# Attention with norms: the activations transposed by transfers and VectorE instead of TensorE

## The chip, the cores and the metric

The kernel runs on one core of a Trainium2 chip. The core has TensorE (PE; its weight loads are listed apart, as PEld), VectorE (DVE), ScalarE (ACT), GpSimd (POOL) and SyncE (SP), whose queue issues all of this kernel's transfers; 16 DMA engines carry them out. SBUF is the on-chip memory of 128 partitions, PSUM the accumulators that TensorE writes. The metric is the device time of one execution in microseconds, as the median of several.

## What is computed

Input `x` is (8, 2048, 512) in float32: 8 sequences of 2048 tokens with 512 features. Of the reference, this is what matters:

```python
N, S, E, H = (4, 2048, 512, 16)
def proj(W, b):
    y = jnp.einsum('nse,fe->nsf', x, W) + b
    return y.reshape(n, s, h, d).transpose(0, 2, 1, 3)
scores = jnp.einsum('nqhd,nkhd->nhqk', Q, K) * scale
attn = jax.nn.softmax(scores, axis=-1)
out = jnp.einsum('nhql,nlhd->nqhd', attn, V)
out = out.reshape(n, s, e)
return jnp.einsum('nse,fe->nsf', out, Wo) + bo
...
x = x + _layernorm(_L0_attn_ref(_layernorm(x, axis=-1), L0_attn_Wq, ...), axis=-1)
x = x + _layernorm(_L0_ffn_ref(_layernorm(x, axis=-1), L0_ffn_attn_mask, ...), axis=-1)
```

Q, K and V come out of `proj` with the heads ahead of the tokens, so the einsums let the 16 heads of a token attend to each other, for each token by itself. In the second line an expert layer gives each of its 16 experts `s_len // n_head` tokens, which is 8 // 16 = 0 for this shape, so what is left of it is a norm with gain `ln_g` and shift `ln_b`. The change touches the beginning alone: x is normed over its features and turned, so that the features lie on the partitions, as the products with Wq, Wk and Wv need it.

## The kernel before

**Units and steps.** The 16384 tokens are worked through in 32 units of 512 tokens, each of 4 tiles of 128 tokens (`NU`, `NT`, `Q4`). Unit `u` has four steps `c` = 0 to 3. While the softmax, the weighing with V and the output rows of unit `u` (and the rows of `u - 1`) are computed, the products q, k and v of unit `u + 1` are made and x of the unit after that is prepared.

**The order is written out by hand.** `STEPS` (lines 692 to 701) has a string for each step, `FIRST_STEPS` (703 to 709) those of the first unit; `step` (712) goes through the items from left to right and each issues its instructions. Every engine, SP's queue with them, executes its own instructions in that order, each when what it waits for is there. The waits follow from the tiles: a tile of a pool with `bufs` buffers takes the place of an older one when all that read the older one is done. The first unit has its own list (`first_unit`, 597), the last one too (`LAST`, 774).

**x before the products.** `lx` loads a tile of 128 tokens (`load_x`, line 243); `xs` takes its mean and variance on VectorE and the reciprocal root on POOL (`stat_x`, 183/184 and 190/191); `xn` norms it on VectorE and sets the last feature to 1 on POOL (`norm_x`, 260/261); `px` turns it in four 128 x 128 transposes on TensorE into a PSUM bank (`turn_x`, 267); `xa` copies the bank into `xb` on ScalarE (`keep_x`, 279/281); `xt`, for the third and fourth tile of a unit, makes four differences, two on VectorE and two on POOL (`add_x`, 290 to 293). `xb` holds seven operands of a product scheme with seven products in place of eight.

**The products.** `q1` to `q7`, `k1` to `k7`, `v1` to `v7` (`multiply`, 317) and `d1` to `d7` for the output (`out_multiply`, 507) are eight matmuls each. Products 1, 6, 7 and 4 of a letter add up in one PSUM bank ("a"), and between them the bank is copied out as it stands: `1e`, `6e`, `7e`, `4e` (`collect` 331 to 350 on ScalarE, `out_collect` 516 on ScalarE and 519 on VectorE). Products 5 and 3 share another bank, and 2 has its own; `2e`, `5e`, `3e` (353, 521) are on VectorE. `w` items write a part to DRAM by SP (`write`, 364/367), from where `sq`, `sk`, `sv` read it back in another layout into qd, kx and vd (376, 382).

**The softmax in a step.** `mx` takes the maximum and the difference on VectorE (404, 406) and the exponential on ScalarE (414); `dn` the sum and its reciprocal on VectorE (419, 420) and the scaling on POOL (421); `tr` transposes 32 x 32 blocks on VectorE (426); `x0` to `x3` place it in `ex` on ScalarE (431); `sc` and `av` are the small products of TensorE at the end of a step (393, 442); `ok` copies the weighed values out (453), `ou` lays the mask (133).

**The rows in a step.** `lr` loads residual rows r by SP (469) for the next step's `ra`; `rs` at the end of a step takes the sum of squares on ScalarE (543) and the reciprocal root on POOL (190/191) for the next step's `ra`; `ra` (552), `rv` (moments of r), `rg` (562), `rf` (566) and `rt` (moments) follow on VectorE, the roots on POOL; `re` takes an offset on VectorE (577), norms on ScalarE (584) and adds on POOL (588); `st` stores by SP (589). `sB` and `sA` are sums on POOL (476 to 480), `ds` seeds a bank on ScalarE (494).

Step 1 before, as an example of the strings:

```python
        "lx lr q6 q6e mx ra dn ok ou q5 rv q7 tr q7e x0 x1 x2 x3 k1 rg rf q5e k1e rt q4 xs q3 q4e re k2 q3e xn"
        " q5w q4w rs px st xa q3w k2e sc av",
```

## Time and profile before

| | |
|---|---|
| three runs | 1883.60, 1885.58, 1885.72 us; median 1885.58 |
| profiled execution | span 1882.1 us from its first to its last instruction; no time of its own beside the span is listed |
| TensorE | 98% busy; 24,026 matmuls |
| VectorE, ScalarE, GpSimd | 76%, 62%, 55% busy |
| clock granted to TensorE | 0.995 of full speed on average |
| DMA | 63% of the 16 engines' time; 312.58 MB in 370,051 packets |
| x's transposes (line 267) | 512 on TensorE, 281 ns each as a row |
| x's norms (line 260) | 128 on VectorE, 740 ns each |
| x's copies (279, 281) | 64 of 595 ns and 64 of 503 ns on ScalarE |
| x's differences (290 to 293) | 128 of some 420 ns on VectorE, 128 of some 737 ns on POOL |

A row of the profile's groups names a line, an engine, an operation and what it writes and reads, then how often it ran, its busy time in all and the mean of one in ns, and at its end the engine's idle time just before and who ended it. A matmul's end is modelled, so two that follow each other overlap in the rows; what one costs the path is read from the chain of work that ended last, which gives each piece the time until the next. A transfer's row on SP is its issue alone; the time to landing is listed apart. In the view by stage each line is a stretch of time: its length, then each engine's busy time and (x) number of instructions in the order PE, PEld, DVE, ACT, POOL, then the granted clock, the DMA engines' busy share and GB/s.

### The profile page before, as it was taken

To read this page: it belongs to the slowest core of one execution; us is meant where nothing else is said; L and a number is where in the kernel's file an instruction comes from. 1 tells how busy PE (TensorE), PEld (TensorE's weight loads), DVE (VectorE), ACT (ScalarE), POOL (GpSimd) and SP (SyncE) were. 2 spreads that over 40 slices of the span, in tenths; PEclk is the share of its full clock that TensorE was granted. 3 is DMA by queue.
4 is the path that set the end of the run, shared out by engine and by line. 5 is a ranking of instruction groups with operands and counts; after the bars stand their busy time and mean duration, and the time that the engine had idled before them with its cause. 6 is when DMAs were issued, how large, how long until landed. Compare 5 with 4: busy or idle time off the path is not lost.

```text
span 1882.1 us, 57927 instructions
## 1 busy us (share of the span) xinstructions
PE 1847.4 (98%) x24026; PEld 1596.9 (85%) x24026; DVE 1423.8 (76%) x2634; ACT 1172.4 (62%) x1910; POOL 1028.9 (55%) x1785
## 2 busy tenths in 40 slices
PE   8999999999999999999999999999999999999994
PEld 7888888888888888888888888888888888888872
DVE  7667777777777777777777777777777777777777
ACT  2556566666666665666666666566666656666666
POOL 5345654555554565555556545555545555455546
PEclk9999999999999999999999999999999999999998
DMA  7765766566766657665667665576556677656671
GB/s 218 187 158 154 186 174 162 152 167 166 181 169 161 166 147 191 175 162 150 171 157 185 172 163 161 154 181 180 161 158 168 157 189 193 165 147 163 154 186 57
DMA packets 370051, 312.58 MB, mean 166 GB/s; under 512 B 149750, under 2 KB 280825, under 8 KB 365564
## 3 DMA queue, kind: packets, MB, share of 16 engines
q1 hardware_dynamic: 369788, 308.89, 63.0%
q8 instruction: 188, 3.08, 0.7%
q14 instruction: 75, 0.61, 0.1%
HBM read 174.59 MB, written 135.27 MB: 165 GB/s over the span
## 4 chain that ended last, share of the span: by engine, by line
PE 93%; POOL 2%; DVE 1%; ACT 1%; DMA 1%; issue 1%; SPq 0%; POOLq 0%; ACTq 0%; DVEq 0%
PE paq L317 12%; PE pak L317 12%; PE pav L317 11%; PE pad L507 11%; PE pk L317 9%; PE pq L317 9%; PE pv L317 9%; PE pd L507 8%; PE sa L393 6%; PE sa L442 4%; PE px L267 3%; ACT ex L431 1%; POOL rs_d L191 1%; POOL e L421 0%; POOL rs_d L190 0%
## 5 line engine op out<-in xcount | busy, mean ns | idle before, releaser
L431 ACT COPY ex<-eT 32x512 f32<-32x512 f32 x512 | 315.5, 616 | 40.1 <-DVE eT L426 31.2
L421 POOL TENSOR_TENSOR e<-e,den 128x512 f32<-128x512 f32 x128 | 134.6, 1052 | 323.2 <-DVE den L420 265.4
L191 POOL TENSOR_TENSOR rs_d<-rs_d,nhalf 128x1 f32<-128x1 f32 x384 | 211.1, 550 | 32.0
L588 POOL TENSOR_TENSOR a<-a,r 128x512 f32<-128x512 f32 x120 | 181.7, 1514 | 44.1 <-ACT a L584 27.0
L190 POOL TENSOR_SCALAR rs_d<-mv_d 128x1 f32<-128x1 f32 x250 | 50.1, 200 | 255.9 <-DVE mv_d L184 242.8
L404 DVE TENSOR_REDUCE top<-sa 128x16 f32<-128x512 f32 x128 | 88.7, 693 | 103.5 <-PE sa L442 66.7
L584 ACT ACTIVATE a<-a,nm,rs_d 128x512 f32<-128x512 f32 x120 | 97.7, 814 | 97.2 <-DVE nm L577 97.2
L414 ACT ACTIVATE e<-e 128x512 f32<-128x512 f32 x128 | 80.8, 631 | 122.7 <-DVE e L406 122.5
L453 ACT COPY oT<-sa 128x512 f32<-128x512 f32 x124 | 134.4, 1084 | 31.8 <-PE sa L442 29.6
L260 DVE TENSOR_SCALAR x<-x,mv_x,rs_x 128x512 f32<-128x512 f32 x128 | 94.7, 740 | 53.5 <-POOL rs_x L191 52.8
L419 DVE TENSOR_REDUCE den<-e 128x16 f32<-128x512 f32 x128 | 87.2, 681 | 62.9 <-ACT e L414 62.8
L393 PEld LDWEIGHTS sa<-kx,qd 64*32 64x32 f32 x8192 | 109.2, 139 | 29.9 <-issue 27.7
L133 ACT COPY sa<-under 128x1024 f32<-128x1024 f32 x129 | 131.7, 1021 | 2.1
L426 DVE STREAM_TRANSPOSE eT<-e 128x512 f32<-128x512 f32 x128 | 91.0, 711 | 54.7 <-POOL e L421 54.7
L393 PE MATMUL sa<-kx,qd 64*32 64x64 f32 x8192 | 129.1, 249 | 1.0 <-DMA vs<-cv 0.9
L543 ACT ACTIVATE junk<-a 128x512 f32<-128x512 f32 x120 | 84.1, 701 | 71.7 <-DVE a L521 71.7
L442 PE MATMUL sa<-ex,vd 64*32 64x64 f32 x8192 | 123.2, 226 | 3.9 <-ACT ex L431 3.4
L317 PE MATMUL paq<-xb,sq 128*128 128x256 f32 x512 | 124.2, 386 | 0.1
L317 PE MATMUL pak<-xb,sk 128*128 128x256 f32 x512 | 124.2, 386 | 0.0
L317 PE MATMUL pv<-wv,xb 128*128 128x256 f32 x512 | 124.1, 385 | 0.0
L317 PE MATMUL paq<-xb,wq 128*128 128x256 f32 x512 | 123.2, 384 | 0.7 <-ACT xb L281 0.4
L317 PE MATMUL pav<-wv,xb 128*128 128x256 f32 x512 | 121.2, 380 | 1.0 <-ACT u3v L337 1.0
(163 smaller groups left out, 4719.8 us busy)
## 6 DMA issues: line engine op xcount, KB each, us to landing
qs<-cq SPq DMA_DIRECT2D x128, 256.0 KB, 2.3
qd<-qs SPq DMA_DIRECT2D x128, 256.0 KB, 5.3
ks<-ck SPq DMA_DIRECT2D x128, 256.0 KB, 2.4
kx<-ks SPq DMA_DIRECT2D x128, 256.0 KB, 4.3
vs<-cv SPq DMA_DIRECT2D x128, 256.0 KB, 3.1
vd<-vs SPq DMA_DIRECT2D x128, 256.0 KB, 4.4
r<-in_x_dram SPq DMA_DIRECT2D x128, 256.0 KB, 4.9
x<-in_x_dram SPq DMA_DIRECT2D x124, 256.0 KB, 4.5
```

Source lines behind the costliest of these rows:

```text
L133: nc.scalar.copy(sa, under.unsqueeze(1).to_broadcast([P, 2, UT]))
L191: nc.gpsimd.tensor_tensor(rs, rs, nhalf, ALU.pow)
L260: nc.vector.tensor_scalar(xs[t], xs[t], mv[:, 0:1], rs, ALU.subtract, ALU.mult)
L317: nc.tensor.matmul(ps[:, 256 * m : 256 * m + 256], lhsT=left[:, e, P * m : P * m + P], rhs=right[:, e, :], start=(n in (1, 2, 5) and m == ...
L393: nc.tensor.matmul(sa[32 * i : 32 * i + 32, t, 64 * rh : 64 * rh + 64], lhsT=qd[u][d].rearrange("p h (b m) -> p (h b) m", b=2)[:, :, m], r ...
L421: nc.gpsimd.tensor_tensor(e, e, den.unsqueeze(2).to_broadcast([P, 16, 32]), ALU.mult)
L431: nc.scalar.copy(ex[q, :, i % 2, :], sm["t"][q])
L442: nc.tensor.matmul(o[:, J], lhsT=vd[u][d, 4 * c + rh, J, :], rhs=ex[d, 8 * (J // 2) + 2 * rh + J % 2].rearrange("p i k -> p (i k)"), start ...
L453: nc.scalar.copy(dst, sa[:, :, 256:].rearrange("p t (k h R) -> p t k h R", k=Q4, h=Q4))
L507: nc.tensor.matmul(ps[:, m], lhsT=left[:, e, P * m : P * m + P], rhs=right[:, e], start=(n in (2, 5) and m == 0 and e == 0), stop=(e == 1) ...
L584: nc.scalar.activation(a, a, AF.Identity, bias=nm, scale=rs)
L588: engine.tensor_tensor(a, a, res.pop((u, k)), ALU.add)
```

## The change

x is no longer turned by TensorE, but for the first unit's four tiles. `load_x` deals the 256 tokens of two tiles out in blocks of 32, `norm_x` norms on ScalarE into a lasting tile `xn` (four places; the last feature stays 1 from the start; an offset is taken on POOL first), the new `move_x` (item `xm`) moves a pair of tiles by four transfers from SBUF to SBUF so that each quarter of the features comes to 32 partitions, and `turn_x` (`px`) now is one VectorE transpose of 32 x 32 blocks for the pair, straight into `xb`. The target of the transfers, `px[h]`, is in a pool with one buffer. The differences are taken for 256 tokens at once, in items of their own: `xt` on VectorE, `xp` on POOL. In a unit after the first, `xs` and `xn` of a tile run in every step, two steps before where they ran; `xm` is the first item of step 1 and follows `sk` in step 3; `px` is in step 1, behind `q4`, and in step 2, behind `rt`; in step 1 the transfers of pair `h + 1` stand ahead of the transpose of pair `h`. `q2` in step 0 moves from behind `rf` to behind `d2e`, `sv` to the front of step 0, `xs` to behind `tr`. The features' new order goes into the weights' rows on the host. The kernel asks for less scratch for dynamic transfers.

```diff
+    mpool = ctx.enter_context(tc.tile_pool(name="mpool", bufs=1))
...
+    xn = const.tile([P, 2, 2, E], F32, name="xn")
...
     def load_x(t):
         if t < NT:
             xs[t] = xpool.tile([P, E], F32, tag="x", name=f"x_{t}")
             n, s = divmod(P * t, S)
-            nc.sync.dma_start(xs[t], x[n, s : s + P, :] if t < NT - Q4 else renumbered[t % Q4])
+            if t < Q4:
+                nc.sync.dma_start(xs[t], x[n, s : s + P, :])
+                return
+            s -= P * (t % 2)
+            J = t % Q4 - t % 2
+            src = x[n, s : s + 2 * P, :] if t < NT - Q4 else renumbered[J : J + 2].rearrange("J p e -> (J p) e")
+            nc.sync.dma_start(xs[t], src.rearrange("(b i t) e -> i t b e", b=Q4, i=2)[t % 2])
...
+    def normed(t):
+        return xn[:, t // 2 % 2, t % 2]
+    def norm_first(t):
+        mv, rs = xrs.pop(t)
+        nc.vector.tensor_scalar(
+            normed(t).rearrange("p (k a e) -> p a k e", k=EC, a=Q4),
+            xs.pop(t).rearrange("p (a k e) -> p a k e", k=EC, a=Q4),
+            mv[:, 0:1], rs, ALU.subtract, ALU.mult,
+        )
+        nc.gpsimd.memset(normed(t)[:, E - 1 : E], 1.0)
     def norm_x(t):
         if t < NT:
             mv, rs = xrs.pop(t)
-            nc.vector.tensor_scalar(xs[t], xs[t], mv[:, 0:1], rs, ALU.subtract, ALU.mult)
-            nc.gpsimd.memset(xs[t][:, E - 1 : E], 1.0)
-    def turn_x(t):
-        if t < NT:
-            px[t] = ps_pj.tile([P, EC, P], F32, tag="pj", name=f"px_{t}")
-            for ec in range(EC):
-                nc.tensor.transpose(px[t][:, ec, :], xs[t][:, ec * P : (ec + 1) * P], ident)
-            del xs[t]
-    def keep_x(t):
-        if t < NT:
-            u, J = divmod(t, Q4)
-            if J == 0:
-                xb[u] = pool2.tile([P, 7, 2, 2 * P], F32, tag="xb", name=f"xb_{u}")
-            j = slice(P * (J % 2), P * (J % 2) + P)
-            if J < 2:
-                dst = xb[u][:, 0:2].rearrange("p n e t -> p (n e) t")[:, :, j]
-                nc.scalar.copy(dst, px[t])
+            nm = small.tile([P, 1], F32, tag="nm", name=f"nmx_{t}")
+            nc.gpsimd.tensor_scalar(nm, mv[:, 0:1], rs, -1.0, ALU.mult, ALU.mult)
+            nc.scalar.activation(
+                normed(t)[:, 0 : E - 1], xs.pop(t)[:, 0 : E - 1], AF.Identity, bias=nm, scale=rs
+            )
+    def begin_x(u):
+        if u not in xb:
+            xb[u] = pool2.tile([P, 7, 2, 2 * P], F32, tag="xb", name=f"xb_{u}")
+        return xb[u]
+    def turn_first(t):
+        px[t] = ps_pj.tile([P, EC, P], F32, tag="pj", name=f"px_{t}")
+        for ec in range(EC):
+            nc.tensor.transpose(px[t][:, ec, :], normed(t)[:, P * ec : P * ec + P], ident)
+    def keep_first(t):
+        dst = begin_x(0)[:, 2 * (t // 2) : 2 * (t // 2) + 2].rearrange("p n e t -> p (n e) t")
+        nc.scalar.copy(dst[:, :, P * (t % 2) : P * (t % 2) + P], px.pop(t))
+    def move_x(h):
+        if h < NT // 2:
+            px[h] = mpool.tile([P, Q4, 2, P], F32, tag="xm", name=f"xm_{h}")
+            for a in range(Q4):
+                src = xn[:, h % 2, :, P * a : P * a + P]
+                nc.sync.dma_start(px[h][32 * a : 32 * a + 32].rearrange("p b i e -> p (b i e)"), src)
+    def turn_x(h):
+        if h < NT // 2:
+            n = 2 * (h % 2)
+            dst = begin_x(h // 2)[:, n : n + 2].rearrange("p n e (c t) -> p (n e) c t", t=32)
+            nc.vector.transpose(dst, px.pop(h).rearrange("p b i (k e) -> p k (b i) e", k=EC))
+    def add_x(u, engine, j=slice(0, 2 * P)):
+        if u < NU:
+            b11, b21, t1, b22, t2, t3, t4 = (xb[u][:, n, :, j] for n in range(7))
+            if engine is nc.vector:
+                nc.vector.tensor_tensor(t3, b22, t1, ALU.subtract)
+                nc.vector.tensor_tensor(t1, t1, b11, ALU.subtract)
             else:
-                nc.scalar.copy(xb[u][:, 2, :, j], px[t][:, 2:4])
-    def add_x(t):
-        if t < NT and t % Q4 >= 2:
-            u, J = divmod(t, Q4)
-            j = slice(P * (J % 2), P * (J % 2) + P)
-            b11, b21, b22, t1, t2, t3, t4 = (xb[u][:, n, :, j] for n in range(7))
-            b12 = px[t][:, 0:2]
-            nc.vector.tensor_tensor(t3, b22, b12, ALU.subtract)
-            nc.vector.tensor_tensor(t1, b12, b11, ALU.subtract)
-            nc.gpsimd.tensor_tensor(t2, b22, t1, ALU.subtract)
-            nc.gpsimd.tensor_tensor(t4, b21, t2, ALU.subtract)
+                nc.gpsimd.tensor_tensor(t2, b22, t1, ALU.subtract)
+                nc.gpsimd.tensor_tensor(t4, b21, t2, ALU.subtract)
...
-        right = xb[u][:, {1: 0, 2: 1, 3: 2, 4: 6, 5: 3, 6: 4, 7: 5}[n]]
+        right = xb[u][:, {1: 0, 2: 1, 3: 3, 4: 6, 5: 2, 6: 4, 7: 5}[n]]
...
     STEPS = (
-        "lx lr sv st ok sB px mx xa q1 q1e ra d2 ou dn d2e rv d6 d6e tr d5 x0 x1 x2 x3 d7 d7e rg rf q2 rt d5e xs"
-        " d4 q2e re xn d4e d3 d3e rs q2w st sc av",
-        "lx lr q6 q6e mx ra dn ok ou q5 rv q7 tr q7e x0 x1 x2 x3 k1 rg rf q5e k1e rt q4 xs q3 q4e re k2 q3e xn"
-        " q5w q4w rs px st xa q3w k2e sc av",
-        "lx lr k6 k6e mx ra dn ok ou k5 rv k7 tr k7e k2w x0 x1 x2 x3 v1 sq rg k5e rf v1e rt k4 xs k4e k5w k3 re xn"
-        " k3e k4w rs px st xa xt k3w sc av",
-        "sk lx lr v2 mx v2e ra v6 ok v6e dn ou ds v5 rv sA v7 tr x0 x1 v7e x2 x3 d1 rg rf v5e v2w d1e v4 rt xs"
-        " v4e v5w v3 re xn v3e v4w rs px xa xt v3w sc av",
+        "sv lx lr st ok sB mx q1 q1e ra d2 ou dn d2e q2 q2e rv d6 d6e tr xs d5 x0 x1 x2 x3 d7 d7e rg rf rt d5e"
+        " d4 q2w xn re d4e d3 d3e rs st sc av",
+        "xm lx lr q6 q6e mx ra dn ok ou q5 rv q7 tr xs q7e x0 x1 x2 x3 k1 rg rf q5e k1e rt q4 px q3 q4e xn re k2 q3e"
+        " q5w q4w rs st q3w k2e sc av",
+        "lx lr k6 k6e mx ra dn ok ou k5 rv k7 tr xs k7e k2w x0 x1 x2 x3 v1 sq rg k5e rf v1e rt px k4 k4e k5w k3 xn re xt"
+        " k3e k4w xp rs st k3w sc av",
+        "sk xm lx lr v2 mx v2e ra v6 ok v6e dn ou ds v5 rv sA v7 tr xs x0 x1 v7e x2 x3 d1 rg rf v5e v2w d1e v4 rt"
+        " v4e v5w v3 xn re v3e v4w rs v3w sc av",
     )
 
     FIRST_STEPS = (
-        "lx sv mx q1 q1e dn ok ou q2 q2e q6 q6e tr k1 k1e x0 x1 x2 x3 q7 q7e q2w lb xs q5 q5e xn q4 q4e px q5w q4w lo"
-        " xa sc av",
-        "lx k2 mx k2e dn ok ou c4 q3 tr k6 k6e x0 x1 x2 x3 q3e k2w q3w k5 xs cs k7 k7e c0 k5e xn px k5w xa sc av",
-        "lx mx v1 v1e dn ok ou k4 k4e k3 k3e tr k4w k3w sq c1 v2 x0 x1 x2 x3 v2e xs c2 c3 v6 v6e xn wt px xa xt v2w sc av",
-        "sk lx ds v7 v7e mx v5 v5e dn ok ou xs tr v4 v4e xn x0 x1 x2 x3 d1 sA v4w v5w d1e px v3 v3e xa xt v3w lg sc av",
+        "lx lx sv mx q1 q1e dn ok ou px q2 q2e xt xp q6 q6e xs tr k1 k1e x0 x1 x2 x3 q7 q7e q2w xn lb xs q5 q5e xn q4 q4e"
+        " q5w q4w lo sc av",
+        "xm lx k2 mx k2e dn ok ou c4 q3 tr k6 k6e x0 x1 x2 x3 q3e k2w q3w k5 xs cs k7 k7e c0 k5e xn k5w sc av",
+        "xm lx lx mx v1 v1e dn ok ou k4 k4e k3 k3e tr k4w k3w sq c1 px v2 x0 x1 x2 x3 xs v2e xs xn c2 c3 v6 v6e xn wt v2w"
+        " sc av",
+        "sk xm lx ds v7 v7e mx v5 v5e dn ok ou px xs tr v4 v4e xn x0 x1 x2 x3 d1 sA v4w v5w d1e v3 v3e xt xp v3w lg sc av",
...
-            "xs": lambda: stat_x(s + 9), "xn": lambda: norm_x(s + 9), "px": lambda: turn_x(s + 8),
+            "xs": lambda: stat_x(next(x_stat)), "xn": lambda: norm_x(next(x_norm)), "xm": lambda: move_x(next(x_move)),
+            "px": lambda: turn_x(next(x_turn)),
...
-            "xa": lambda: keep_x(s + 8), "xt": lambda: add_x(s + 8),
+            "xt": lambda: add_x(next(x_add), nc.vector), "xp": lambda: add_x(next(x_last), nc.gpsimd),
...
-    x_tiles = iter(range(11, 2 * NT))
+    x_tiles, x_stat, x_norm = (iter(range(n, 2 * NT)) for n in (11, 9, 9))
+    x_move, x_turn = (iter(range(n, NT)) for n in (4, 3))
+    x_add, x_last = (iter(range(1, 2 * NU)) for _ in range(2))
...
-    nc = _bacc.Bacc("TRN2", target_bir_lowering=False, num_devices=1)
+    nc = _bacc.Bacc("TRN2", target_bir_lowering=False, num_devices=1, dynamic_dma_scratch_size=1024)
...
+        if m != "o":
+            w = w.reshape(512, 4, 4, 32).transpose(0, 2, 1, 3).reshape(512, 512)
```

The first unit's list changes to match: its first four tiles keep TensorE and a ScalarE copy (`turn_first`, `keep_first`), the next four take the new way (`move_x(2)` behind `spread_qk(0, "k")`, `turn_x(2)` and `move_x(3)` behind `v7e`), and `stat_x(8)` moves ahead of `v5`.

More of the change, by code (lines that the diff above doesn't have):

```diff
@@ L611, in first_unit @@
         stat_x(1)
-        norm_x(0)
-        turn_x(0)
-        keep_x(0)
+        norm_first(0)
+        turn_first(0)
+        keep_first(0)
         stat_x(2)
-        norm_x(1)
-        turn_x(1)
-        keep_x(1)
+        norm_first(1)
+        turn_first(1)
+        keep_first(1)
         stat_x(3)
-        norm_x(2)
-        turn_x(2)
-        keep_x(2)
-        norm_x(3)
-        turn_x(3)
-        keep_x(3)
+        norm_first(2)
+        turn_first(2)
+        keep_first(2)
+        norm_first(3)
+        turn_first(3)
+        keep_first(3)
         for t in range(4, 8):
@@ L631, in first_unit @@
         less_last("q", nc.vector, (0,))
-        add_x(2)
+        for engine in (nc.vector, nc.gpsimd):
+            add_x(0, engine, slice(0, 128))
         less_last("q", nc.vector, (1,))
-        add_x(3)
+        for engine in (nc.vector, nc.gpsimd):
+            add_x(0, engine, slice(128, 256))
         nc.gpsimd.memset(ex, 0.0)
@@ L657, in first_unit @@
         spread_qk(0, "k")
+        move_x(2)
         stat_x(6)
         run(0, "v2 v2e v2w v6 v6e")
-        turn_x(4)
-        keep_x(4)
         norm_x(6)
-        turn_x(5)
         stat_x(7)
@@ L666, in first_unit @@
         run(0, "v7 v7e")
-        keep_x(5)
         load_x(9)
         norm_x(7)
-        turn_x(6)
-        keep_x(6)
+        turn_x(2)
         load_x(10)
-        add_x(6)
-        turn_x(7)
-        keep_x(7)
+        move_x(3)
+        stat_x(8)
         run(0, "v5 v4 v5e v4e v4w v5w")
-        stat_x(8)
-        add_x(7)
         run(0, "v3 v3e v3w")
```

## The prediction

> **What bounds the kernel now.** I read the busy shares first, then the chain of work that ended last, then the busy time by stage and the timeline of one unit in the steady middle.

> ```profile
> span 1882.1 us, 57927 instructions
> PE 1847.4 (98%) x24026; PEld 1596.9 (85%) x24026; DVE 1423.8 (76%) x2634; ACT 1172.4 (62%) x1910; POOL 1028.9 (55%) x1785
> PE 93%; POOL 2%; DVE 1%; ACT 1%; DMA 1%; issue 1%; SPq 0%; POOLq 0%; ACTq 0%; DVEq 0%
> ```

> TensorE is the path. The next view gives the four steps of one unit (span, then busy time and instructions of each engine, clock, DMA share): TensorE is busy for all of every step, at full clock. Between 400 and 1600 us the waits of TensorE come to one, of 0.2 us. So what leaves TensorE comes off the time, as long as nothing else becomes late.

> ```profile
> 904.18:920.13 15.95, 15.95 (x196) 13.83 (x196) 12.33 (x24) 8.75 (x15) 10.70 (x18) 1.00 0.63 159
> 920.13:934.46 14.33, 14.33 (x189) 12.58 (x189) 10.86 (x20) 9.38 (x16) 5.29 (x11) 1.00 0.30 93
> 934.46:947.05 12.59, 12.59 (x189) 11.05 (x193) 8.61 (x17) 8.57 (x13) 4.08 (x10) 1.00 0.80 212
> 947.05:961.39 14.34, 14.34 (x197) 12.59 (x202) 12.18 (x24) 9.73 (x17) 11.51 (x18) 1.00 0.85 212
> ```

> The profiled execution shows its span alone, 1882.1 us; the three runs have 1883.6 to 1885.72, so 1.5 to 3.6 us lie around it. I add changes to the median, 1885.6.

> **What goes from TensorE.** The chain by time prices a turned tile (start, length, what):

> ```profile
> 905.78 0.59 PE px L267 x4
> 906.37 1.73 PE paq L317 x8
> ...
> 934.09 0.44 PE px L267 x4
> ```

> Three tiles of a unit cost 0.44; the one behind the softmax products 0.59, of which 0.19 comes back, since a product that follows those takes 1.92 and not 1.73. That is 3 x 0.44 + 0.40 = 1.72 us a unit. Units 1 to 29 turn 116 tiles (49.9 us); the eight tiles turned in the first unit give 3.5. Saving: 53.4 us.

> A transpose row lasts 273 to 281 ns, but four advance the path by 0.44. [...]

> **What it costs elsewhere, by amount.** Each unit, VectorE loses four norms (0.74) and four small subtractions (0.42) and gets two transposes (0.71 for 512 columns; 1024 against 512 columns adds 0.53 in the two-operand rows, 1.22 against 0.69; so 1.24) and two subtractions of 512 (0.69): -4.6 + 3.9. ScalarE loses 2 x 0.59 + 2 x 0.50 of copies and gets four norms, priced by L584, the same form, 0.81: +1.0. POOL loses 4 x 0.12 and 4 x 0.73 and gets 4 x 0.30 (L579) and 2 x 1.27: +0.3. SP gets 8 issues of about 0.47 (four vd issues take 1.88). The moves add 63,488 packets of 512 B; at the 51 ns that a packet takes on average (63% of 16 engines' 1882 us over 370,051 packets) that is at most 11 points of DMA share. Not shown before are the wide transpose (between one 512 row, 0.71, and two, 1.42), the norm on ScalarE (between L543, 0.70, and L584) and the transfer from SBUF to SBUF (between qs, 2.3 us to landing, and qd, 5.3). All this fits into the idle time above (VectorE 13.2 of 57.2 us a unit, ScalarE 20.8, POOL 25.6), and the price by amount is nothing; without that cover it would be ScalarE's 1.0. The order is another matter.

> [...]

> **What it costs by order.** Steps begin, by the chain, at 904.18, 920.20, 934.53, 947.05; "into step n" counts from there.

> (a) *Step 0, product d4.* q2 stood between d7 and d4; it goes ahead of d6, so d4 follows d7 in the same bank and must wait until ScalarE has copied the bank out (d7e). The first unit shows this hand-over, with two tiles' transposes in between:

> ```profile
> 41.26 1.89 PE L317 MATMUL pav<-sv,xb 128*128 128x256 f32 x8
> 43.23 0.59 ACT L334 COPY u2v<-pav 128x512 f32<-128x512 f32 x1 [4.60 <-PE pav L317]
> 43.87 1.99 PE L317 MATMUL pav<-sv,xb 128*128 128x256 f32 x8
> ```

> From the product's end (43.15) to the next one's start 0.72; back to back they overlap by 0.16. Price 0.9 (0.7 to 1.1 with the slower restart), 30 times. In the first unit v6 and v7 lose this cover too: 0.9 once.

> (b) *Step 1, q3.* The next tile's moments (0.81 of VectorE) move ahead of q5e, which ended at 929.92; q3, which needs it, starts at 930.64. It ends 0.1 late; with the hand-over 0.2 (0 to 0.5).

> (c) *Step 1, SP.* In step 1 the four transfers of the next pair stand first in SP's queue, but their target is the only buffer, and its old content is read by the transpose that VectorE reaches after rt, late in the same step. So SP waits, and the loads of x and r stand behind. rt ends 10.53 into step 1; the moved moments make it 11.34, the transpose ends at 12.58, four issues end at 14.46, x takes 0.6, r is issued at 15.06 and lands 4.9 later (median; 3.1 to 7.2) at 19.96. The shorter step 1 lasts 14.1, so r is there 5.86 into step 2. Before:

> ```profile
> 935.90 0.60 SPq L469 DMA_DIRECT2D r<-in_x_dram  x1
> 937.43 0.74 DVE L552 SCALAR_TENSOR_TENSOR r<-a,rs_d,r 128x512 f32<-128x512 f32 x1
> 939.17 0.69 DVE L419 TENSOR_REDUCE den<-e 128x16 f32<-128x512 f32 x1 [0.99 <-ACT e L414]
> 942.93 0.68 DVE L353 TENSOR_TENSOR ck<-pk,u3k 128x512 f32<-128x512 f32 x1
> 944.73 1.89 PE L317 MATMUL pk<-xb,wk 128*128 128x256 f32 x8
> ```

> (That r serves step 3; the one for step 2 was issued at 921.35.) VectorE needs it at 2.90 into step 2, and behind it in the same queue stand den, the softmax transpose and k5e, which k3 on TensorE waits for. ra starts at 5.86, den at 6.54 where it was 4.64: 1.90 late. k5e ended at 9.08; plus 0.81 plus 1.90 is 11.79, where k3 would start at 10.36. Price 1.45 with the hand-over; a landing of 3.1 makes it 0, one of 7.2 makes it 3.7.

> (d) *Step 2, POOL.* The two subtractions of a pair now stand as one block of 2 x 1.27 ahead of rs, whose reciprocal root ra of step 3 needs. rt ends 2.29 after k5e's start: 13.40. POOL's root takes 0.91 (14.31), the norm's offset 0.30, ScalarE's norm 0.81 and its output norm 0.81 (16.2), POOL's residual add 1.27, the block 2.55, rs 0.82: 20.9. Step 2 now lasts 12.09 + 1.45, so that is 7.35 into step 3, where ra started at 4.19. The 3.16 pass down VectorE's queue to the softmax transpose and on ScalarE to v7e (ended 9.64, now 12.80), and v4, due at 10.45, waits 2.35. Without (c) the same sum gives 1.86; POOL's add at its slowest row, 1.8, makes it 3; with the norm off this chain it falls to 0.7.

> Moved and covered: x's statistics and norms come two steps sooner on tiles that are loaded two steps before; the transfers of step 1 land by 5.7 into step 2 (14.46 + 5.3 - 14.1) and are turned at 13.4; vd's issues pass x and r in step 0, so that r lands about 12 into step 0 and is needed 3 into step 1; kx waits for the later k3w and lands about 12.8 into step 3, before its use at 16. If step 3 weren't lengthened by (d), 1.1 of that cover would be left. The larger of the DMA's costs is in the landing range of (c).

> In the first unit one more x load stands ahead of vd, on which its first weighing waits: within 1 us, taken as 0. The host's new order of weight rows costs nothing on the chip, and the last unit is the same.

> Sum for units 1 to 29: -1.72 + 0.9 + 0.2 + 1.45 + 2.35 = +3.18; x 29 = 92.2. Unit 30: +0.9. First unit: -3.5 + 0.9. Total +90.5, so **1976 us**.

> **Rivals.**
> - *r comes in time* (quieter queue than the median, or room in step 2): only (a), (b), (d) at 1.86. +1.24 x 29 - 1.7 gives 1920. For it: step 1 has a DMA share of 0.30, and the r loads issued in it landed in 4.2 us. Against: the loads stand behind 0.75 MB just issued.
> - *Faster: VectorE's order has room.* The place is ra in steps 2 and 3. If r lands by 4.0 into step 2 and POOL's rs is done by about 5 into step 3, den isn't held and k3 and v4 are on time; (a) and (b) remain: -0.62 x 29 - 1.7, 1866. For it: VectorE idles 13 of 57 us a unit. Against: my rows miss both points by 1.9 and 2.3 us.
> - *All hidden*: 1885.6 - 53.4 = 1832. It needs d4 not to wait for d7e, though both use one bank.
> - *Worse*: (c) at 3.7 and (d) at 3: +6.1 a unit, 2060.
> - The transposes do leave TensorE; a time near 1885 would mean that stalls of 1.7 a unit took their place.

> **Numbers.** About 0.2% (3.8 us) is what a measurement of this kernel can tell from no change. Forecast 0.50 (1940 to 2010), r in time 0.18, room 0.13, all hidden 0.09, worse 0.07, near 1885 0.03. Faster 0.22, within 0.2% 0.03, slower 0.75. The range leaves out all-hidden and the worst: 1862 to 2010.

> **What would show it.** Right: SP waiting in each step 1 for the transpose of the moved tile; the r load issued after the end of step 1; VectorE idle before ra (L552) in step 2 for r's DMA and in step 3 for POOL's root; TensorE waiting for ScalarE before d4 and v4 and for VectorE before k3; px near 0.1% of the chain. Wrong: TensorE without gaps in steps 2 and 3, or r issued as early as before.

## The result, and the profile after

Before 1884.59 us (four runs, 1883.57 to 1885.72), after **2053.24 us** (four runs, 2050.04 to 2059.08): ratio 1.09, 95% interval 1.0882 to 1.0918. The forecast was 1976, the range 1862 to 2010: the direction was right, the size was not. The lines of the page that answer to those of before:

```profile
span 2049.8 us, 57097 instructions
PE 1857.3 (91%) x23523; PEld 1547.5 (75%) x23530; DVE 1398.8 (68%) x2510; ACT 1191.9 (58%) x1910; POOL 1059.5 (52%) x1723
PE 43%; DVE 19%; POOL 12%; DMA 8%; issue 6%; ACT 6%; SPq 5%; POOLq 0%; DVEq 0%; ACTq 0%
```

TensorE has 496 transposes less to do (503 fewer in the records, of which some are missing) and still is the busiest engine, but no longer the path alone: its share of the chain that ended last falls from 93% to 43%, and VectorE, POOL, the transfers and SP's queue hold 44%. No engine has become the bound; all of them are idle more than before. The same unit by stage (columns as before):

```profile
991.42:1008.26 16.84, 16.16 (x194) 13.44 (x193) 10.81 (x21) 10.28 (x16) 10.51 (x17) 1.00 0.80 205
1008.26:1022.55 14.29, 14.15 (x185) 11.99 (x184) 10.62 (x19) 9.64 (x16) 4.87 (x12) 1.00 0.07 25
1022.55:1036.67 14.12, 12.53 (x177) 10.54 (x177) 9.06 (x17) 7.71 (x13) 5.12 (x10) 1.00 1.04 258
1036.67:1053.06 16.39, 14.17 (x185) 12.00 (x185) 12.41 (x22) 9.23 (x15) 12.17 (x17) 1.00 0.97 198
1098.75:1116.82 18.07, 15.86 (x185) 13.19 (x184) 12.56 (x23) 10.03 (x17) 12.97 (x19) 0.91 0.98 202
```

TensorE now waits 0.7 us in step 0, 1.6 in step 2, 2.2 in step 3. The DMA share of step 1 is 0.07: SP stands in its queue. The last line is step 3 of another unit, 1.7 us longer at a lower clock; more on that below. TensorE's waits over the run (total, times, longest) are headed by the three that the prediction named, v4 on u3v, k3 on k5e and d4 on d7e; the fourth line is the longest wait of SP's queue, that of the transfers (L308):

```profile
PE pav L350 <- ACT u3v L370: 61.9, 30, 2.4
PE pk L350 <- DVE ck L386: 49.1, 29, 2.4
PE pad L540 <- ACT a L549: 20.3, 30, 0.7
SPq L308 <- DVE nm L610: 354.4, 29, 19.4
```

In the changed kernel L308 is a transfer of x, L315 the VectorE transpose that reads what the transfers brought, L252 and L502 the loads of x and r, L585 ra, L452 den, L386 q, k and v's VectorE sums, L621 the row's add, L325/326 the block xp, L350 and L540 the products. The timeline of the unit above (start, length, engine, line) shows the two longer waits from end to end:

```profile
1019.66 1.25 DVE L315 STREAM_TRANSPOSE xb<-xm 128x1024 f32<-128x1024 f32 x1
...
1020.97 2.67 SPq L308 DMA_DIRECT2D xm<-xn  x4
...
1024.35 0.61 SPq L502 DMA_DIRECT2D r<-in_x_dram  x1
...
1029.09 0.75 DVE L585 SCALAR_TENSOR_TENSOR r<-a,rs_d,r 128x512 f32<-128x512 f32 x1 [3.30 <-DMA r<-in_x_dram]
1029.76 0.68 DVE L452 TENSOR_REDUCE den<-e 128x16 f32<-128x512 f32 x1
...
1034.01 0.69 DVE L386 TENSOR_TENSOR ck<-pk,u3k 128x512 f32<-128x512 f32 x1
...
1034.75 1.99 PE L350 MATMUL pk<-xb,wk 128*128 128x256 f32 x8 [1.59 <-DVE ck L386]
...
1039.10 1.28 POOL L621 TENSOR_TENSOR a<-a,r 128x512 f32<-128x512 f32 x1 [1.64 <-ACT a L617]
1040.33 1.27 POOL L325 TENSOR_TENSOR xb<-xb 128x512 f32<-128x512 f32 x1
1041.68 1.27 POOL L326 TENSOR_TENSOR xb<-xb 128x512 f32<-128x512 f32 x1
...
1043.31 0.55 POOL L193 TENSOR_TENSOR rs_d<-rs_d,nhalf 128x1 f32<-128x1 f32 x1
1043.90 0.75 DVE L585 SCALAR_TENSOR_TENSOR r<-a,rs_d,r 128x512 f32<-128x512 f32 x1 [2.20 <-POOL rs_d L193]
...
1049.41 1.99 PE L350 MATMUL pav<-wv,xb 128*128 128x256 f32 x8 [2.22 <-ACT u3v L370]
```

First (c): SP begins the four transfers only 12.7 us into step 1, when the transpose of the pair before has ended (the line of SP's waits names nm, a short VectorE instruction that ends 0.04 after it), r is issued 1.8 into step 2 and VectorE is idle until it lands, then den and k5e follow and k3 starts late. Then (d): POOL does the row's add and the block of two before the root that ra needs, ra starts 7.2 into step 3, v4 2.2 late.

By place in the run the 167.7 us of the two spans are: first unit and what is before it +18.5, units 1 to 29 +148.4, unit 30 +0.9, the end 0.

### The profile page after: what moved, and what is told of

Read it like the earlier page. It is cut to its first block, busy times and chain, and to the rows that moved or that the text cites. A ratio compares the mean times of both kernels' runs of the same rounds, so it can differ in the third digit from the quotient of the medians.

```text
span 2049.8 us, 57097 instructions
## 1 busy us (share of the span) xinstructions
PE 1857.3 (91%) x23523; PEld 1547.5 (75%) x23530; DVE 1398.8 (68%) x2510; ACT 1191.9 (58%) x1910; POOL 1059.5 (52%) x1723
## 4 chain that ended last, share of the span: by engine, by line
PE 43%; DVE 19%; POOL 12%; DMA 8%; issue 6%; ACT 6%; SPq 5%; POOLq 0%; DVEq 0%; ACTq 0%
PE pad L540 8%; PE pd L540 8%; PE paq L350 6%; DMA r<-in_x_dram 6%; PE pv L350 5%; POOL e L454 5%; PE sa L426 4%; SPq L308 4%; PE pav L350 3%; DVE eT L459 3%; DVE den L452 3%; PE pq L350 3%; PE sa L475 3%; PE pk L350 2%; DVE r L585 2%
## 5 line engine op out<-in xcount | busy, mean ns | idle before, releaser
L621 POOL TENSOR_TENSOR a<-a,r 128x512 f32<-128x512 f32 x120 | 155.6, 1297 | 194.6 <-ACT a L617 194.6
L585 DVE SCALAR_TENSOR_TENSOR r<-a,rs_d,r 128x512 f32<-128x512 f32 x120 | 91.4, 762 | 161.6 <-DMA r<-in_x_dram 99.4
L284 ACT ACTIVATE xn<-x,nmx,rs_x 128x511 f32<-128x511 f32 x124 | 100.7, 813 | 156.7 <-POOL nmx L283 155.8
L350 PE MATMUL pav<-wv,xb 128*128 128x256 f32 x512 | 130.2, 399 | 61.9 <-ACT u3v L370 61.9
L350 PE MATMUL pk<-xb,wk 128*128 128x256 f32 x512 | 125.8, 389 | 49.1 <-DVE ck L386 49.1
L350 PEld LDWEIGHTS pav<-wv,xb 128*128 128x128 f32 x512 | 97.4, 195 | 86.4 <-ACT u3v L370 73.9
L350 PEld LDWEIGHTS pk<-xb,wk 128*128 128x128 f32 x512 | 95.8, 192 | 72.9 <-DVE ck L386 60.7
L350 PE MATMUL pv<-wv,xb 128*128 128x256 f32 x512 | 133.0, 405 | 5.3 <-DVE cv L386 4.0
L540 PE MATMUL pad<-wo,oT 128*128 128x256 f32 x480 | 116.5, 386 | 20.3 <-ACT a L549 20.3
L350 PE MATMUL paq<-xb,sq 128*128 128x256 f32 x512 | 125.7, 389 | 4.7 <-POOL xb L325 3.7
L350 PE MATMUL pav<-sv,xb 128*128 128x256 f32 x512 | 123.0, 384 | 5.4 <-ACT u2v L367 4.0
```

Of the source, the lines that this page charges most:

```text
L284: nc.scalar.activation(normed(t)[:, 0 : E - 1], xs.pop(t)[:, 0 : E - 1], AF.Identity, bias=nm, scale=rs)
L350: nc.tensor.matmul(ps[:, 256 * m : 256 * m + 256], lhsT=left[:, e, P * m : P * m + P], rhs=right[:, e, :], start=(n in (1, 2, 5) and m == ...
L540: nc.tensor.matmul(ps[:, m], lhsT=left[:, e, P * m : P * m + P], rhs=right[:, e], start=(n in (2, 5) and m == 0 and e == 0), stop=(e == 1) ...
L585: nc.vector.scalar_tensor_tensor(r, y, rs, r, ALU.mult, ALU.add)
L621: engine.tensor_tensor(a, a, res.pop((u, k)), ALU.add)
```

## The experiments

Theory: the order alone costs the time, through those three waits. Rival 1: the added transfers (32.5 MB, 63,488 packets) slow the traffic. Rival 2: the added work of VectorE, ScalarE and POOL can't be hidden. Diffs show pieces of the strings of `STEPS`; each kernel does the whole computation unless it says otherwise.

**The three placements, one by one and together.**

```diff
e_xm, step 1
- xm lx lr q6
+ lx lr q6
- rt q4 px q3
+ rt q4 px xm q3
e_q2, step 0
- d2e q2 q2e rv
+ d2e rv
- rg rf rt d5e d4 q2w
+ rg rf q2 rt d5e d4 q2e q2w
e_rs, step 2
- k3e k4w xp rs st
+ k3e k4w rs xp st
```

e_xm: 

> Step 1's four transfers stand behind the transpose px instead of at the front, so nothing stands behind their wait in SP's queue; they start as late as before. Theory (three waits that the order makes: d4 on d7e, k3 through the late r, v4 through POOL's block ahead of rs): the wait of k3 (49.1 us over the run, 29 times) goes, with some 0.2 us of restart each, and v4's wait loses 0.5 each; with half of the half-clock windows that is 1975 us (1960 to 2000); r is issued about 1.5 into step 1 and VectorE's wait for r's DMA (99.4 us) goes. Rival 1 (the added transfers themselves, 32.5 MB in 63,488 packets, slow the memory traffic): the same bytes move, 2040 or more. Rival 2 (the added work of VectorE, ScalarE and POOL is the cost): 2045 to 2055.

e_q2: 

> q2 stands between d7 and d4 again. Theory: TensorE's wait for d7e (20.3 us, 30 times 0.7) goes, with 0.2 us of restart each: 2027 us (2015 to 2035). If one cause carries nearly all (the late r or POOL's block): 2045 to 2055. Rivals 1 and 2: 2045 to 2055.

e_rs: 

> In step 2 rs stands ahead of POOL's two subtractions xp. Theory: rs is 2.5 us earlier, ra in step 3 starts near 4.7 us and not 7.2, v7e is in time and v4's wait (61.9 us, 30 times, with 0.2 of restart) goes: 1980 us (1965 to 1995). If the late r carries nearly all, v4 is late all the same: 2040 or more. Rivals 1 and 2: 2045 to 2055.

e_all: 

> The three edits together. Theory: the three waits and the half-clock windows go, what is left is the saving of 53 us and about 0.2 us a unit for q3: 1840 us (1832 to 1860). Rival 1 (transfers): over 1900. Rival 2 (amount of work): over 1885.

Measured: e_xm 1991.63 (ratio 1.0568, 1.0552 to 1.0584), e_q2 2045.31 (1.0853, 1.0835 to 1.0871), e_rs 2007.28 (1.0647, 1.0619 to 1.0676), **e_all 1933.47** (1.0256, 1.0240 to 1.0272). The waits of k3 and d4 are gone where their edits took them away; v4's falls from 61.9 us to 17.4 in e_rs. Steps (c) and (d) are real: 62 and 46 us. But all four stay short of the theory: 78 and 73 us were expected of these two, moving q2 back gave 8 where 26 were expected, and the three together stop 93 us above the theory's figure, on the rivals' side. The waits of e_q2 (the first line) and of e_all (the other two) tell why: other waits stood behind those that went.

```profile
PE pad L540 <- POOL oS L510: 10.5, 15, 0.7
```

```profile
PE pad L540 <- POOL oS L510: 16.1, 23, 0.7
PE pav L350 <- ACT u3v L370: 12.1, 27, 1.0
```

In e_q2: between d2 and d6 q2 had covered POOL's sums sB, which are late themselves (in step 0 the copy of the weighed values, their source, waits for ScalarE's tail of the step before). So the place of q2 was paid for on one side and earned on the other. In e_all v4 still waits, since xt stands ahead of the maximum in step 3.

**Rival 1 by itself.** The kernel before, with as many transfers, about where the change has them:

```diff
b_moves
+    def move_more(h):
+        for a in range(Q4):
+            src = yn[:, h, :, P * a : P * a + P]
+            nc.sync.dma_start(ym[32 * a : 32 * a + 32].rearrange("p b i e -> p (b i e)"), src)
step 1
- q5w q4w
+ q5w ym q4w
step 3
- sk lx lr
+ sk ym lx lr
```

> The kernel before, with the change's eight transfers from SBUF to SBUF a unit added (in step 1 behind q5w, in step 3 behind sk) from a lasting tile of zeros into a tile that nobody reads; nothing waits for them. Rival 1 (the transfers themselves cost the time that the three edits left, 1933 against 1832): 1930 to 1990. Theory (order alone): 1886 (1882 to 1895).

Measured: 1891.96, ratio 1.0036 (1.0023 to 1.0049). The page of this run:

```profile
PE 1845.9 (98%) x24019; PEld 1600.5 (85%) x24026; DVE 1422.9 (75%) x2634; ACT 1171.6 (62%) x1910; POOL 1029.5 (55%) x1786
q1 hardware_dynamic: 435068, 340.36, 74.8%
```

The transfers raise the DMA share from 63% to 75% and cost 7.3 us. Rival 1 is out: the load is small, what hangs on it is not.

**Moving on through the order.** Each of the next kernels adds to the one before.

```diff
e_g = e_all, and (the first unit's second xp goes, as step 0 has it)
- k3 xn re xt k3e
+ k3 xn re k3e
- k4w rs xp st
+ k4w rs st
- v3e v4w rs v3w
+ v3e xt v4w rs v3w
- d2e rv d6
+ d2e rv xp d6
e_gf = e_g, and in steps 1, 2 and 3
- xn re k2 q3e q5w q4w rs st
+ rs xn re k2 q3e q5w q4w st
- k4e k5w k3 xn re k3e k4w rs st
+ k4e rs k5w k3 xn re k3e k4w st
- sA v7 tr
+ sA rs v7 tr
- xt v4w rs v3w
+ xt v4w v3w
e_best = e_gf, and in step 1 (in the first unit px goes behind the softmax transpose, xm behind px)
- tr xs q7e
+ tr q7e
- rt q4 px
+ rt xs q4 px
e_h = e_best, and (the first unit's third xm goes, as step 0 has it)
- sk xm lx lr
+ sk lx lr
- sv lx lr st ok
+ sv lx lr st xm ok
e_hk = e_h, and in step 3
- rv sA rs v7 tr xs x0
+ rv sA v7 tr x0
- v4 rt v4e v5w v3 xn re
+ v4 rt rs xs v4e v5w v3 re xn
e_hkl = e_hk, and in step 0
- rv xp d6 d6e tr xs d5
+ rv d6 d6e tr xs xp d5
```

e_g: 

> The three edits together, and the differences of x moved: xt from the end of step 2 to behind v3e of step 3, POOL's xp to step 0 behind rv. With the three edits TensorE still waits for u3v before v4 (12.1 us, 27 times), since xt stands ahead of the maximum on VectorE in step 3, and for POOL's sums before d6 (16.1 us, 23 times), since xp, two-input adds of 2.9 us, pushes the sums, the roots and with them ScalarE's copy of the weighed values into step 0. Theory: both waits and 0.1 to 0.3 of restart each go: 1895 us (1885 to 1910). Rival 1 (transfers) and rival 2 (amount of work): 1925 or more, since the same work is done.

e_gf: 

> As the kernel of the run before, and rs of steps 1 to 3 moved out of the tail of the step (step 1: ahead of xn; step 2: behind k4e; step 3: behind sA), so that ScalarE's copy of the weighed values in the next step does not queue behind it. Theory: ScalarE's tail of 0.9 us leaves step 0, top starts 0.6 to 0.9 earlier there, 0.1 to 0.3 a unit: 1888 us (1878 to 1900). Rivals 1 and 2: no change against the run before.

e_best: 

> As the kernel of the run before; xs of step 1 back behind rt, so that q5e is not late; and in the first unit xm and px of steps 2 and 3 as in the steady units, px behind the softmax transpose and xm behind px. Theory: q3's lateness (0.3 with restart 0.4 a unit, 29 times) goes, 12 us; of the first unit's 18 us over before, 8 to 15: together 1863 us (1850 to 1875), faster than before by over 0.5%. Rival 1 (transfers): over 1900. Rival 2 (amount): over 1885.

e_h: 

> As the last kernel, with the four transfers of step 3 moved to step 0 of the next unit, behind the store, so that vs is not issued behind them. In the last kernel vs takes up to 4.6 us to issue at the turn of the unit, an instruction load of 16 KB starts late there, and TensorE stands still in the middle of its small products with nothing that it waits for (13.7 us in 4 stalls, up to 5.0 each, a half-clock window behind most). Theory (crowded transfers at the turn of the unit hold instruction loads, vs and vd): these stalls and their half-clock windows (about 20 to 25 us together) go, the mean of step 0 falls from 17.4 to 16.5: 1878 us (1870 to 1888). If the stalls come from elsewhere: 1900. Rival 2 (amount of work): 1900.

e_hk: 

> As the kernel of the run before, with the order of step 3 as in the kernel before the change: xs behind rt, re ahead of xn, and rs behind rt. Theory: POOL's root of rt no longer queues behind the roots of rs and x, so re and xn leave ScalarE by about 2.0 into step 0 and its copy of the weighed values follows at 2.0 where it now starts at 2.8; top at 3.1 instead of 3.9, d6 and d2 are not held (0.4 each): 0.7 to 0.9 a unit, 20 to 26 us: 1854 us (1846 to 1866). Rival 2: no change against the run before.

e_hkl: 

> As the kernel of the run before, with POOL's xp in step 0 behind the root of xs instead of ahead of it, so that rg and rf (1.39 and 1.57 us beside it, 0.72 and 0.76 alone) are not slowed and d5e, which d3 waits for (0.2 us, 14 times), is earlier. Theory: 0.1 to 0.2 a unit, 3 to 6 us: 1850 us (1843 to 1862). Rival 2: no change.

Measured: e_g 1911.21 (ratio 1.0140), e_gf 1910.51 (1.0142), e_best 1902.19 (1.0092, 1.0063 to 1.0120), e_h 1890.19 (1.0035, 1.0022 to 1.0048), e_hk 1916.29 (1.0171), e_hkl 1905.05 (1.0118). All six missed the range expected of them, and mostly for one reason: a wait that goes lets the next one show. e_g: v4's wait is gone, d6's (14.0 us) is not. e_gf: d6's is gone and the time is the same, which is what the rivals expected; in its place TensorE stands 5.9 us ahead of d2 and 9.1 in the small products for nothing that the view of the waits shows, nearly all of it in step 0, and 5.3 at the start of unit 1 for what the profile names as a transfer of x. In e_best steps 1 to 3 have no wait left in most units (medians 13.90, 12.15, 13.90), but step 0 lasts 16.55 and up to 22.7. One of its stalls:

```profile
1320.40 0.83 PE L475 MATMUL sa<-ex,vd 64*32 64x64 f32 x58
...
1320.68 4.62 SPq L397 DMA_DIRECT2D vs<-cv  x2
...
1326.28 0.24 PE L475 MATMUL sa<-ex,vd 64*32 64x64 f32 x1 [5.05 <-issue]
```

One small product of 64 is left, all its inputs are there, and TensorE stands for 5 us while SP takes 4.6 us to issue two stores of vs. In the trace an instruction load of 16,384 bytes begins at 1323.89, takes 0.9, and TensorE goes on 1.5 after it. Past the first 125 us the 18 profiles have 58 stalls of TensorE of over 1 us with no releaser ("issue"), and in all 58 TensorE goes on 1.27 to 1.69 us after the end of such a load; of its 284 other waits of that length 11 do. So I read these stalls as waits for instructions; the view of the waits names no releaser for them. Moving step 3's transfers away from there (e_h) took 12 us off and the longest such stall from 5.0 to 2.6: the loads behind the three long ones in the small products begin 1.25 to 2.66 us after TensorE has stopped in e_best, and within 0.2 of its stopping in e_h. That crowded data transfers hold the loads back fits this, but what a load waits for is in no trace, so that part is argued and not shown.

e_hk went the wrong way, by 26 us, with a wait that was new:

```profile
PE pd L540 <- ACT oT L486: 25.6, 24, 1.2
```

With re ahead of xn, POOL's queue had the row's add (it waits for ScalarE's norm, 13.3 to 14.1 into step 3) ahead of the offset that x's norm waits for; that norm ran 3.4 into step 0 and ScalarE's copy oT behind it at 4.2. One item issues work to three queues, and moving it for one of them moved it in the others. e_hkl took off 11: beside POOL's block rg and rf had taken 1.39 and 1.57 us, away from it 0.72 and 0.76.

**All the work, in an order that hides it.** From e_h:

```diff
e_fit
     def stat_x(t):
+            nc.gpsimd.tensor_scalar(nm, mv[:, 0:1], rs, -1.0, ALU.mult, ALU.mult)
     def norm_x(t):
-            nc.gpsimd.tensor_scalar(nm, mv[:, 0:1], rs, -1.0, ALU.mult, ALU.mult)
step 3
- sk lx lr v2
+ sk lx lr st v2
- sA rs v7 tr xs x0
+ sA v7 tr x0
- v4 rt v4e v5w v3 xn re
+ v4 rt xs rs v4e v5w v3 re xn
step 0
- rv xp d6 d6e tr xs d5
+ rv d6 d6e tr xs xp d5
step 2
- k4w st k3w
+ k4w k3w
first unit
- turn_x(2) load_x(10) move_x(3) stat_x(8) run(v5 to v4w) run(v3 v3e v3w)
+ load_x(10) run(v5 to v4w) stat_x(8) run(v3 v3e v3w) turn_x(2) move_x(3)
- lx lx sv mx q1
+ sv lx lx mx q1
- xp q6 q6e xs tr k1 k1e
+ xp k1 k1e q6 q6e xs tr
- xn c2 c3 v6 v6e xn
+ c2 c3 v6 v6e xn xn
```

> From the kernel with step 3's transfers moved (1890), not from the two after it, in which TensorE waits for ScalarE's copy of the weighed values before d2 (24 to 26 us, 24 times): re's add on POOL stood there ahead of the norm's offset. Now that offset follows its root at once (made with the statistics), step 3 has rt, xs, rs, then re ahead of xn; xp in step 0 stands behind the root of xs; step 2's store goes to step 3, behind the loads, so that ks is not issued behind a wait for POOL's add. In the first unit the transpose of the first moved pair stands behind v3e, k1 ahead of q6, v6e ahead of the norms, sv first. Theory (queues alone, each engine's own order): the copy oT starts by 1.8 us into step 0 (2.8 now), top by 3.0 (3.9); step 0 from 16.9 to 15.9 (1.0 x 29 = 29 us); first unit 8 to 12 us: 1850 us (1842 to 1866), faster than before by 1.0 to 2.2%. Rival 2 (the added work of VectorE, ScalarE and POOL can't be hidden): 1885 or more.

Measured: **1854.72 us**, ratio 0.9845 (0.9828 to 0.9861): inside the range expected, and faster than both kernels, with the changed kernel's data flow and amount of work. Rival 2 is out for units 1 to 29; the first unit, with what is before it, still ends 11.3 us later than in the kernel before. Its page's engine shares, and one unit by stage:

```profile
PE 91%; DMA 3%; DVE 2%; ACT 1%; POOL 1%; issue 1%; SPq 0%; POOLq 0%; DVEq 0%; ACTq 0%
```

```profile
895.00:910.62 15.62, 15.62 (x194) 13.60 (x193) 12.55 (x22) 9.45 (x14) 12.31 (x19) 1.00 0.94 214
910.62:924.51 13.89, 13.89 (x185) 12.07 (x184) 10.55 (x19) 9.75 (x17) 6.08 (x13) 1.00 0.25 74
924.51:936.67 12.16, 12.16 (x178) 10.55 (x177) 9.52 (x17) 8.52 (x15) 5.51 (x9) 1.00 1.02 252
936.67:950.57 13.90, 13.90 (x185) 12.08 (x184) 11.09 (x21) 10.07 (x16) 9.31 (x15) 1.00 0.96 235
```

TensorE is busy in all of every step of this unit again, 55.57 us where before had 57.21: the chain's price of x's transposes, 1.72, was nearly right (1.64). In the mean of units 1 to 29, with some longer steps 0 among them, it is 1.46.

**Each placement put back alone** into this kernel (in f_d and f_h the item's place in the first unit goes back too):

```diff
f_a, step 0
- d2e rv
+ d2e q2 q2e rv
- rg rf q2 rt d5e d4 q2e q2w
+ rg rf rt d5e d4 q2w
f_c, step 1
- lx lr q6
+ xm lx lr q6
- px xm q3
+ px q3
f_d, steps 2, 3 and 0
- k4e rs k5w k3 xn re k3e k4w k3w
+ k4e k5w k3 xn re xt k3e k4w xp rs k3w
- v3e xt v4w
+ v3e v4w
- xs xp d5
+ xs d5
f_h, steps 3 and 0
- sk lx lr
+ sk xm lx lr
- st xm ok
+ st ok
```

f_a: 

> The last kernel (1855) with one part of the change put back: q2 in step 0 behind d2e, not between d7 and d4. Theory (step (a) of the prediction at its own price, which the run with q2 moved back could not show since d6 then waited for POOL's sums): d4 waits for d7e, 0.7 and 0.2 of restart, 29 times: 1880 us (1874 to 1888). If the hand-over is covered now that ScalarE is early: 1855 to 1860.

f_c: 

> The last kernel with the four transfers of step 1 at the front of the step again. Theory (step (c)): SP waits for the transpose, r lands about 5.9 into step 2 and ra starts near 6.5 instead of 3.0, den near 7.2 instead of 4.8, so k5e ends at 12.1 where k3 is due at 10.3: 1.8 and 0.1 to 0.2 of restart, 29 times, with some half-clock windows: 1912 us (1900 to 1930). If r in time doesn't matter: 1855 to 1862.

f_d: 

> The last kernel with xt and POOL's block xp back at the end of step 2 and rs behind the block, as the change had them. Theory (step (d)): ra in step 3 starts near 7 instead of 4.3, v4 waits for u3v about 2, with restart and some half-clock windows 2.0 to 2.6 a unit: 1922 us (1905 to 1940). If POOL's place doesn't matter: 1855 to 1862.

f_h: 

> The last kernel with step 3's transfers at the front of step 3 again (and the first unit's third pair moved in its own step 3). Theory (crowded transfers at the turn of the unit): vs is issued late and slowly, vd and an instruction load with it: 1868 us (1860 to 1882), with TensorE standing in the small products for nothing that the trace shows. If that crowding needed the other waits too: 1855 to 1860.

Measured: f_a 1882.76 (ratio 0.9994, 0.9985 to 1.0004), f_c 1930.77 (1.0248, 1.0231 to 1.0265), f_d 1907.93 (1.0122, 1.0107 to 1.0137), f_h 1860.95 (0.9871, 0.9857 to 0.9886). The three waits, one in each run, of f_a, f_c and f_d:

```profile
PE pad L543 <- ACT a L552: 20.3, 30, 0.7
```

```profile
PE pk L353 <- DVE ck L389: 62.2, 29, 3.4
```

```profile
PE pav L353 <- ACT u3v L373: 47.7, 29, 2.0
```

Each brings its own wait and no other that comes back unit after unit: +28.0 us for (a) and +53.2 for (d), inside the ranges expected, +76.1 for (c), just above its own. The +6.2 of f_h lie at the low end of the range, without the sign that was expected: the longest stall in its small products with no releaser is 1.3 us, as in e_fit, and of the 5.4 us between the two profiles 2.2 lie before unit 1. So the long stalls of e_best needed more than these transfers in this place. The sum is 163.5 of the 198.5 between 1854.7 and 2053.2. The other 35 must be the smaller moves (xs in step 1, the first unit, the tails of steps 2 and 3) and what the waits do to each other; no run takes them apart.

## Why the prediction was right in kind and too small

The three waits came where the prediction put them. It fell 77 us short, 56 in units 1 to 29 and 21 in the first unit, and three of its steps failed: in (c) the price of an issue, 0.47 where 0.69 was measured, and of the hand-over to the product behind the wait, 0.02 where 0.26 was measured; the clock, taken as full, which cost some 19 us; and the first unit, put at -2.6 where +18.5 was measured. The rest, some 20 us, is spread over (a), (b) and the saving.

Mean step lengths of units 1 to 29: before 16.15, 14.35, 12.52, 14.34; after 17.11, 14.30, 14.26, 16.81; the best kernel 15.90, 13.94, 12.15, 13.91. After less best is what the order costs, by step; the last column is what the time of a kernel with one placement put back has over the best, by 29.

| step of the prediction | predicted, a unit | changed kernel | put back alone |
|---|---|---|---|
| what goes from TensorE | -1.72 | -1.46 (best less before) | |
| (a) step 0, d4 | 0.9 | 1.21, all of step 0 | 0.97 |
| (b) step 1, q3 | 0.2 | 0.36 | |
| (c) step 2, k3 | 1.45 | 2.11 | 2.62 |
| (d) step 3, v4 | 2.35 | 2.90 | 1.83 |
| sum | 3.18 | 5.12 | |
| first unit and before it, once | -2.6 | +18.5 | |

- **By amount: nothing.** Right for units 1 to 29: in e_fit, with all the work, they take 43 us less than in the kernel before (the profiles' steps). The transfers by themselves cost 7.3 us. That the price lies in the order was the decisive sentence.
- **(a)** Right to a tenth when it is alone. The prediction did not see that q2's new place covers sB's lateness in the same step, so that undoing it gives 8 us and not 28.
- **(b)** Mechanism right: q3 starts 0.3 late and slower by 0.1 in e_all, and the step fell from 14.33 to 13.96 when xs went back.
- **(c)** Mechanism right to the instruction; mis-sized was the issue of a transfer, "four issues of about 0.47", a price borrowed from the vd rows. From one issue to the next it takes 0.69 here (2.67 for the four), so r is issued 1.80 into step 2 and not 0.96. ra then starts at 6.55 instead of 5.86 (medians), and k3's wait is 49.1 / 29 = 1.7. The sum has 1.43 for it and 0.02 for the hand-over; but the eight products behind the wait take 1.99 in the chain and not 1.73, so the hand-over is 0.26. Put back alone, the wait is 62.2 / 29 = 2.1, since x's moments stand ahead of the transpose there, and eight half-clock stretches (below) add most of the rest.
- **(d)** Mechanism right. "Without (c) the same sum gives 1.86": alone it was 1.83 (2.06 more in step 3, less 0.18 in step 0, which is without POOL's block then). With (c), ra starts at 7.2 as worked out (7.35), v4 waits 2.2, and a step 3 without half clock is 2.4 longer than the best kernel's; the half-clock stretches make that 2.90 in the mean.
- **Clock.** "At full clock" was read off the kernel before and kept for the one after. It was not: eleven half-clock stretches of 3.4 us fell into units 1 to 29, eight of them in step 3, where the step lasts 18.07 with one and 16.33 without: 1.74 each, 19 us, about a third of the 56 us that the steady units missed.
- **First unit.** "-3.5 + 0.9" counted the transposes and one bank and did not go through the unit's own list. There q6 waits for xp 3.7 us, v3 behind the first pair's transpose 4.0, v7 for a copy behind x's norms 4.0, and four half-clock stretches at 1.7 make 6.8: 18.5 of the 21 that it missed, by the profile. No run took these apart.
- **Rivals.** The transfer that comes in time (1920) and the order with room (1866) need a different order; with that they are passed (e_fit, 1854.7), while all-hidden (1832) is not reached. "Worse" at 2060, with a chance of 0.07, was the nearest, but by luck in part: it had (d) right with 3 a unit, but (c) at 3.7 where 2.11 was measured, and nothing of the first unit. The range was cut off below it although both upper ends were known.

## What to carry to other kernels

Where the other engines have room, as here, a change that only moves work off the bound engine is priced by order, not amount: go through every queue for each moved item, SP's and POOL's too, and ask what stands behind each wait. Read waits as a stack: taking one away shows the next, so price each placement by putting it back into a version without waits, not by taking it out of one with many. And price pauses of the bound engine twice, for their length and for the clock behind them (here 2.2 us, and 1.74 more where half clock followed).

## What the runs showed of the hardware that was not expected

```profile
1048.03:1051.44 3.41, 2.03 (x9) 1.82 (x10) 3.27 (x7) 2.52 (x5) 3.33 (x4) 1.00 1.23 158
1051.44:1054.86 3.42, 3.42 (x137) 2.85 (x136) 1.34 (x4) 1.49 (x3) 2.14 (x6) 1.00 1.15 264
...
1109.47:1112.88 3.41, 1.40 (x6) 1.25 (x7) 3.27 (x7) 3.05 (x5) 3.33 (x4) 1.00 1.21 156
1112.88:1116.29 3.41, 3.41 (x9) 2.70 (x8) 1.36 (x4) 0.85 (x2) 2.78 (x7) 0.50 1.14 227
```

Both are the same wait of v4, 2.2 us. The first lies across a border of the grid: 1.38 us of idle in the one stretch, 0.84 in that before, and the clock stays. The second lies in one stretch whole: 2.01 us idle, and the next stretch runs at half clock. Over the profiles of all 18 kernels (past the first 125 us) a stretch with over 2.0 us of idle was followed by half clock in 54 of 55 cases, the other being the one in which the products of its run end; one with 1.9 to 2.0 in 19 of 23, one with 1.8 to 1.9 in 2 of 15, and one with less in 4 of some 9,000, all four at half clock already. So the same wait cost 2.2 us, or 3.9 with the 1.74 that a step 3 with half clock lasted longer, by where it fell on the grid: in e_xm v4's waits were shorter (52.1 against 61.9 us) and step 3 longer (17.11 against 16.81), since 18 of its 29 had a half-clock stretch, and in f_d, with waits of up to 2.0 on another phase, one had.

**Issuing was not free, and not constant.** From one transfer of 512 B pieces from SBUF to SBUF to the next SP takes 0.69 us in the changed kernel's median. A store of vs takes it 0.36 us in the median before and at most 1.6; with nothing but the transfers added (b_moves) that becomes 0.64 and 3.8, and in e_best the longest is 4.5.
